# A decoder layer's mixer: heads spread by transfers, column groups filled across two chunks, squares added on GpSimd, the front a stage of its own

## The chip, the cores and the metric

The kernel runs on one core of a Trainium2 chip. The metric is the device time of one execution in microseconds (us). Three runs of the kernel before gave 1148.04, 1148.34 and 1158.81 us, with a median of 1148.34. One more execution was taken with the profiler.

## The reference

The input `x` has 16 batches of 256 positions and 256 channels, all float32. One layer applies three blocks, each followed by a layernorm of the sum with its input.

```python
# 1. mixer (32 heads k of 8 channels; 4 angles theta each)
z = causal_conv4(x @ in_proj_w)                  # x_val 256, gate 256, score 32
p_w = exp(clip(score_scale * z_score, -20, 20)) * time_weight
poly = w0 + w1 * x_val - w2 * x_val**2           # w = softmax(deriv_logits)
phi = x_val * theta
num_re, num_im, den = cumsum over t of p_w*poly*cos(phi), p_w*poly*sin(phi), p_w
re, im = num_re / max(den, 1e-4), num_im / max(den, 1e-4)
rs = rsqrt((sum(re**2) + sum(im**2)) / 64 + 1e-5)     # one per head and position
y = re*rs*norm[:32] @ W_re + im*rs*norm[32:] @ W_im
x = layernorm(x + (y * silu(z_gate)) @ out_proj_w)
# 2. attention by autocorrelation: 256-point spectra of q, k, v (16 heads), the
#    best delays of the mean correlation, softmax over them, v rolled and summed
x = layernorm(x + attn(x, ctx) @ Wo + bo)
# 3. feed-forward, a forward and an inverse branch of 8 experts of rank 64
h = gelu(q @ router_w1.T + b1); weights = softmax(h @ router_w2.T + ...)
out = sum_k weights_k * (xV_k * cumsum_t(yW_k)) @ U_k + weights @ b
x = layernorm(x + (fwd + alpha * inv) @ W_O.T)
```

## The kernel before

**Tiling.** Batches go in eight pairs. The mixer works with channels in the partitions and two batches of 256 positions in the free dimension. The feed-forward weights are multiplied together once at the start (`fold_weights`).

**The mixer.** `front` transposes `x`, forms the scores (line 208) and, from them, `pw`, the weight per head and position; heads lie in 16 rows of each 32-row group. It projects `x` in four blocks (line 225) and convolves them into `zcs` on VectorE (`convolve`, line 186). For the two value blocks `m` it builds `g`, the polynomial times `pw`. `pw` has a row for each head, and `g` one for each of 8 channels, so two products with a 0/1 matrix `sel_h` (line 231) copy each head's row to 8 rows of PSUM.

`body` takes each value block `m` in two chunks `h`. For a chunk it spreads channels to four angle rows by transfers (`spread`, line 247), forms sine and cosine in tiles `sn` and `cs`, multiplies by the spread `ge`, and sums over time with scans (`cumsums`, line 120). ScalarE squares both sums into `ge` and `sq` (279, 280). TensorE then forms `y` (line 284: weights of 32 columns, so a product fills one of four column groups of the array; a chunk `h` uses groups 2h and 2h+1) and adds the squares into `ss` (line 289: four groups; one set of products for `ge`, one for `sq`). The tiles `sn`, `cs` and `ge` have two buffers each. After both blocks, `sv`, the inverse of the norm, is copied from heads to channels by `sel_h` again (line 307), multiplied in (308), and projected out (316).

**Attention and feed-forward.** `attention` takes spectra (450), products (473, 484), picks delays in `choose`, rolls (`rolled`, 564, 574). `feed_forward` transposes, sums over time, forms router logits (611, 613, 614), softmax, then eight expert tiles `e` (two products at 661 and 665, a transfer `wb` of the weights, two VectorE multiplies 662 and 666), and at the end multiplies all eight with `u_o` (675) and the bias (676).

**What sets the order.** `run` interleaves generators: each stream has a start time, a length and a number of steps, and the one that is least advanced emits next. `mixer(p)`, body of pair p and then front of pair p+1, fills 70 steps from time p to p+1; attention of p starts at p+1.2, feed-forward at p+2.6. A planner then orders each engine's queue from this priority, its own estimates, and the free buffers; every queue runs in order. Eight pairs share nine `x` buffers. All transfers named here are issued by SyncE (SP).

Of the kernel before, what the change touches and what calls it, by code (L numbers as in the profile page):

```python
# [11 lines left out]
F32 = mybir.dt.float32  # L12
# [7 lines left out]
P = 128  # L20
B, L, D = 16, 256, 256
K, H, M, A = 32, 8, 4, 4
HM = H * M
# [11 lines left out]

A_AT, A_LEN = 0.2, 1.0
# [17 lines left out]
def decoder_kernel(ctx: ExitStack, tc: tile.TileContext, a: dict, out: bass.AP):  # L54
# [45 lines left out]
    sel_h = load("sel_h", [P, 2, D], eng=G)  # L100
# [89 lines left out]

    def front(p, made):
# [30 lines left out]
        for m in range(4):  # L222
            ps = m_bank()
            for c in range(2):
                T.matmul(ps, w_in[:, c, m * P : (m + 1) * P], xT[:, c, :, :], start=c == 0, stop=c == 1)  # L225
            zcs.append(convolve(mx, "zc", split(ps), m, 6))
            if m < 2:
                g = mx.tile([P, 2, L], F32, name="g", tag="g", bufs=3)
                ps = m_bank()
                for j in range(2):  # L230
                    T.matmul(
                        ps[:, j * L : (j + 1) * L], sel_h[:, j, m * P : (m + 1) * P], pw, start=True, stop=True
                    )
                S.activation(g, zcs[m], AF.Identity, bias=dw[:, 1:2], scale=dw[:, 3:4])
                G.tensor_tensor(g, g, zcs[m], ALU.mult)
                V.scalar_tensor_tensor(g, g, dw[:, 0:1], split(ps), ALU.add, ALU.mult)  # L236
                gs.append(g)
            if m < 3:
                yield 4
# [9 lines left out]
    def body(p, made):  # L249
        zcs, gs, den = made.pop(p)  # L250
        ss = y_ps.tile([P, L], F32, name="ss", tag="ss")
        for m in range(2):
            y = y_ps.tile([P, 512], F32, name="y", tag="y")
            for h in range(2):
# [22 lines left out]
                yield 5  # L277
                sq = mx.tile([P, 2, 512], F32, name="sq", tag="sq", bufs=1)
                S.activation(ge, sn, AF.Square)  # L279
                S.activation(sq, cs, AF.Square)  # L280
                for n, part in enumerate((cs, sn)):
                    for i in range(2):
                        q = 32 * (2 * h + i)
                        T.matmul(y[q : q + 32, :], w_ri[:, n, :], part[:, i, :], start=n == 0, stop=n == 1)  # L284
                for n, s in enumerate((ge, sq)):
                    for par in range(2):
                        for j in range(2):
                            q = 32 * (2 * par + j)
                            T.matmul(  # L289
                                ss[q : q + 32, :], ones_bd[:, 4 * m + 2 * h + par, :],  # L290
                                s[:, par, j * L : (j + 1) * L],
                                start=m == 0 and h == 0 and n == 0, stop=m == 1 and h == 1 and n == 1,
                            )
                yield 2
# [8 lines left out]
        for m in range(2):  # L303
            y = zcs[2 + m]
            ps = m_bank()
            for j in range(2):
                T.matmul(ps[:, j * L : (j + 1) * L], sel_h[:, j, m * P : (m + 1) * P], sv, start=True, stop=True)
            V.tensor_tensor(y, y, split(ps), ALU.mult)
# [110 lines left out]
    def mixer(p):  # L419
        if 2 * p + 2 < B:  # L420
            for b in (2 * p + 2, 2 * p + 3):
                if xs[b] is None:
                    load_x(b)
        yield from body(p, made)
        if p + 1 < NP:
            yield from front(p + 1, made)

    with tc.tile_pool(name="fold", bufs=1) as fold:
        for b in range(2, 4):
            load_x(b)  # L430
        run((0, 1, 70, mixer(0)))
# [160 lines left out]
    def feed_forward(p):  # L592
# [14 lines left out]
        for br in range(2):  # L607
            for rb in range(2):
# [3 lines left out]
                h = ff.tile([P, 512], F32, name="h", tag="h", bufs=2)  # L612
                S.activation(h, ps, AF.Gelu, bias=pv[:, C_RB1 + rb : C_RB1 + rb + 1])  # L613
                T.matmul(pl[32 * br : 32 * br + 32, :], w2t[:, rb, :], h, start=rb == 0, stop=rb == 1)  # L614
# [36 lines left out]
        es = []  # L651
        for br in range(2):
            for kb in range(4):
# [4 lines left out]
                e = ff.tile([P, 512], F32, name="e", tag="e", bufs=8)  # L658
# [10 lines left out]
        tiles = []  # L669
        for j in range(2):  # L670
            ps = f_bank()
            for c in range(2):
                o, cut = ps[:, c * D : (c + 1) * D], slice((2 * j + c) * P, (2 * j + c + 1) * P)
                for i in range(8):
                    T.matmul(o, es[i][:, cut], u_o[:, i, :], start=i == 0, stop=False)  # L675
                T.matmul(o, wT[:, cut], b_o, start=False, stop=True)  # L676
                yield 4
            V.tensor_tensor(pair[j], pair[j], split(ps), ALU.add)
            tiles += [pair[j][:, 0, :], pair[j][:, 1, :]]
# [6 lines left out]
    streams = [(p, 1.0, 70, mixer(p)) for p in range(1, NP)]  # L686
# [7 lines left out]
_HEADS = [[4 * cb + i for cb in range(par, 8, 2) for i in range(4)] for par in range(2)]  # L694
# [7 lines left out]
def _shape_constants():  # L702
# [27 lines left out]
    dist_p, sel_h = np.zeros((P, L)), np.zeros((P, 2, D))  # L730
    for q, rows in _score_rows():
        dist_p[rows] = dist[_HEADS[q // 2]]
        for r, k in zip(rows, _HEADS[q // 2]):
            sel_h[r, q % 2, k * H : (k + 1) * H] = 1.0
    c["dist"], c["sel_h"] = dist_p, sel_h
    ones_bd = np.zeros((P, 8, 32))
    for r in range(P):
        for cb in range(8):
            ones_bd[r, cb, 4 * (cb // 2) + r // HM] = 1.0
# [77 lines left out]
```

## Time and profile before

| What | us |
|---|---|
| median of three runs | 1148.34 |
| the profiled execution, its own time | 1144.82 |
| its span | 1143.0 |
| PE busy | 971.6 |
| DVE busy | 718.1 |
| ACT busy | 520.8 |
| POOL busy | 235.1 |

The span runs from the first to the last instruction; the rest of the profiled execution's time lies around it. PE is TensorE's matmuls, PEld its weight loads, DVE is VectorE, ACT is ScalarE, POOL is GpSimd, SP is SyncE. In a group, the line and engine come first, then output and inputs by name, the shape, the count, the busy time, the mean of one in nanoseconds, and the idle time of the engine before them with what ended it. A float32 product appears as two records. In a timeline the start comes first, then the length. Busy time says how long an engine worked and not who was late.

### The profile page before, as it was taken

The page shows a single profiled execution, that of the slowest core. Times are in us where ns is not written, and L with a number is a line of the kernel's source. Part 1 is how long each engine was busy: PE and PEld are TensorE (multiplying, and loading weights), DVE is VectorE, ACT ScalarE, POOL GpSimd, SP SyncE. Part 2 cuts the span into 40 slices and gives each one's busy share as a digit, 9 for nine tenths or more (in the row PEclk, how much of TensorE's full clock was granted, in tenths as well). Part 3 has the DMA queues.
Part 4 walks back from the last instruction along what each step waited for, and adds up shares of the span by engine and source line. Part 5 has one row for each costly group of instructions (what it writes and reads, how often), then busy time and mean ns, then how long its engine had stood idle before and what let it go on. Part 6 is the DMA issues. An engine that isn't in the chain of part 4 may idle for free.

```text
span 1143.0 us, 11089 instructions
## 1 busy us (share of the span) xinstructions
PE 971.6 (85%) x3820; PEld 543.0 (48%) x3820; DVE 718.1 (63%) x1197; ACT 520.8 (46%) x754; POOL 235.1 (21%) x499
## 2 busy tenths in 40 slices
PE   5868848767999788988999899988999799889695
PEld 2335315423547354553547454644456357356344
DVE  4866887865977578855886488855875443243231
ACT  2864774764654373633653474526463311310300
POOL 4102203212211320232112221122013211210100
PEclk9989968979999999998999899999999899989898
DMA  9612313310641143411550155203340050031050
GB/s 319 169 38 60 90 44 66 66 35 1 125 79 37 37 106 43 82 46 23 107 102 10 38 112 81 47 28 78 61 93 19 0 74 1 19 56 19 18 74 19
DMA packets 45512, 72.06 MB, mean 63 GB/s; under 512 B 4448, under 2 KB 18320, under 8 KB 45456
## 3 DMA queue, kind: packets, MB, share of 16 engines
q1 hardware_dynamic: 44240, 68.04, 29.1%
q0 software_dynamic: 1216, 3.31, 0.9%
q8 instruction: 30, 0.49, 0.2%
q14 instruction: 26, 0.21, 0.1%
HBM read 16.81 MB, written 4.19 MB: 18 GB/s over the span
## 4 chain that ended last, share of the span: by engine, by line
PE 49%; DVE 18%; POOL 7%; ACT 7%; issue 6%; DMA 1%; SPq 0%; POOLq 0%; ACTq 0%; DVEq 0%
PE fps L675 10%; PE fps L661 8%; PE fps L665 7%; PE y L284 3%; DVE zc L186 3%; ACT x L177 2%; PE mps L316 2%; DVE cs L120 2%; PE fps L473 2%; PE fps L450 2%; PE ss L289 2%; PE fps L614 2%; PE fps L574 2%; PE fps L611 1%; PE fps L676 1%
## 5 line engine op out<-in xcount | busy, mean ns | idle before, releaser
L661 PE MATMUL fps<-fcT,w_c 128*128 128x512 f32 x256 | 126.2, 617 | 0.0
L665 PE MATMUL fps<-fxT,w_v 128*128 128x512 f32 x256 | 120.4, 592 | 0.0
L675 PE MATMUL fps<-u_o,e 128*128 128x256 f32 x512 | 116.3, 380 | 0.0
L675 PEld LDWEIGHTS fps<-u_o,e 128*128 128x128 f32 x512 | 96.4, 190 | 18.1 <-issue 5.9
L170 POOL TENSOR_TENSOR ln_rs<-ln_rs 128x4 f32<-128x4 f32 x72 | 14.4, 199 | 440.9 <-DVE ln_rs L168 437.1
L177 ACT ACTIVATE x<-x,ln_rs 128x256 f32<-128x256 f32 x96 | 50.0, 592 | 113.6 <-POOL ln_rs L175 113.6
L611 PE MATMUL fps<-fxT,w_h 128*128 128x512 f32 x128 | 66.3, 643 | 18.8 <-ACT fxT L602 18.8
L665 PEld LDWEIGHTS fps<-fxT,w_v 128*128 128x128 f32 x256 | 49.2, 192 | 62.6 <-issue 58.8
L473 PE MATMUL fps<-Wkv,spec 128*128 128x512 f32 x128 | 64.4, 643 | 15.4 <-ACT spec L454 15.4
L186 DVE SCALAR_TENSOR_TENSOR zc<-mps,pv,zc 128x510 f32<-128x510 f32 (+2 forms) x96 | 70.4, 738 | 9.2 <-ACT zc L184 8.7
L120 DVE TENSOR_TENSOR_SCAN sn<-again,sn 128x1024 f32<-128x1024 bf16 x32 | 73.1, 2285 | 0.5
L120 DVE TENSOR_TENSOR_SCAN cs<-again,cs 128x1024 f32<-128x1024 bf16 x32 | 73.1, 2283 | 0.1
L661 PEld LDWEIGHTS fps<-fcT,w_c 128*128 128x128 f32 x256 | 48.4, 197 | 49.5 <-issue 48.6
L225 PE MATMUL mps<-xT,in_proj_w 128*128 128x512 f32 x128 | 68.3, 660 | 4.0 <-DVE g L236 4.0
L490 POOL TENSOR_TENSOR pp<-qf,kf 128x512 f32<-128x512 f32 x16 | 28.2, 1764 | 189.5 <-ACT qf L488 189.5
L279 ACT ACTIVATE ge<-sn 128x1024 f32<-128x1024 f32 x32 | 33.7, 1054 | 71.2 <-DVE sn L120 49.6
L662 DVE TENSOR_TENSOR e<-wb,fps 128x512 f32<-128x512 f32 x64 | 43.7, 682 | 34.3 <-PE fps L661 19.1
L289 PE MATMUL ss<-ge,ones_bd 128*32 128x256 f32 x256 | 47.4, 409 | 19.2 <-ACT ge L279 19.2
L265 ACT ACTIVATE sn<-sn,theta_col 128x512 f32<-128x512 f32 x64 | 45.9, 721 | 36.0 <-DMA sn<-zc 35.8
L666 DVE TENSOR_TENSOR e<-e,fps 128x512 f32<-128x512 f32 x64 | 43.7, 682 | 27.1 <-PE fps L665 25.9
L613 ACT ACTIVATE h<-fps,pv 128x512 f32<-128x512 f32 x32 | 21.2, 681 | 79.9 <-PE fps L611 79.9
L284 PE MATMUL y<-cs,w_ri 128*32 128x512 f32 x128 | 43.6, 660 | 12.8 <-DVE cs L120 11.5
(236 smaller groups left out, 1869.7 us busy)
## 6 DMA issues: line engine op xcount, KB each, us to landing
sn<-zc SPq DMA_DIRECT2D x64, 256.0 KB, 4.7
ge<-g SPq DMA_DIRECT2D x64, 256.0 KB, 4.9
wb<-fwT SPq DMA_DIRECT2D x64, 256.0 KB, 4.4
x<-in_x SPq DMA_DIRECT2D x16, 256.0 KB, 3.3
ct<-in_ctx SPq DMA_DIRECT2D x16, 256.0 KB, 2.7
out<-x SPq DMA_DIRECT2D x16, 256.0 KB, 2.1
in_proj_w<-in_in_proj_w SPq DMA_DIRECT2D x1, 512.0 KB, 6.2
V_fwd<-in_V_fwd SPq DMA_DIRECT2D x1, 512.0 KB, 11.2
```

What stands on the lines that cost most here:

```text
L120: V.tensor_tensor_scan(dst, again[:, : dst.shape[1]], src, 0.0, ALU.mult, ALU.add)
L177: S.activation(t, t, AF.Identity, scale=y[:, i : i + 1], bias=nb[:, i : i + 1])
L186: V.scalar_tensor_tensor(zc[..., s:], ps[..., : L - s], cw[:, 3 - s : 4 - s], zc[..., s:], ALU.mult, ALU.add)
L225: T.matmul(ps, w_in[:, c, m * P : (m + 1) * P], xT[:, c, :, :], start=c == 0, stop=c == 1)
L265: S.activation(sn[:, i, :], sn[:, i, :], AF.Identity, scale=tcol[:, cb : cb + 1])
L284: T.matmul(y[q : q + 32, :], w_ri[:, n, :], part[:, i, :], start=n == 0, stop=n == 1)
L289: T.matmul(ss[q : q + 32, :], ones_bd[:, 4 * m + 2 * h + par, :], s[:, par, j * L : (j + 1) * L], start=m == 0 and h == 0 and n == 0, stop ...
L473: T.matmul(ps, cf[:, c, f * P : (f + 1) * P], wkv[:, c, :], start=c == 0, stop=c == 1)
L611: T.matmul(ps, w_h[:, c, br, rb * P : (rb + 1) * P], xT[:, c, :, :], start=c == 0, stop=c == 1)
L661: T.matmul(pc, w_c[:, c, br, cut], cT[:, c, :, :], start=c == 0, stop=c == 1)
L665: T.matmul(pv_, w_v[:, c, br, cut], xT[:, c, :, :], start=c == 0, stop=c == 1)
L675: T.matmul(o, es[i][:, cut], u_o[:, i, :], start=i == 0, stop=False)
```

## The change

It has five parts.

1. `sel_h` and its four products per value block and pair are gone. `spread_heads` makes four transfers for each block, each taking 8 head rows and writing every row 8 times, into a tile `hs` with two buffers. It serves `pw` in the front and `sv` in the body. The order of heads in the groups (`_HEADS`, `ones_bd`) is changed to suit.
2. The body keeps `cs` and `sn` of both chunks and forms `y` after the second, over four column groups.
3. GpSimd adds the two squares of a chunk, and `ss` has half as many products.
4. Both branches' router projections are formed before their logits, so two logits products on different groups can follow each other; `h` has three buffers in place of two.
5. The front is a stream of its own, from p+0.3 to p+0.95, beside the body of the pair ahead. Besides these, the feed-forward multiplies by `u_o` after each branch of four experts, adding to `x` twice, and `e` has six buffers in place of eight.

```diff
+FRONT_AT, FRONT_LEN = 0.3, 0.65
-    sel_h = load("sel_h", [P, 2, D], eng=G)
+    def spread_heads(src, m):
+        t = mx.tile([P, 2, L], F32, name="hs", tag="hs", bufs=2)
+        for h in range(2):
+            for j in range(2):
+                q = 32 * (2 * (1 - h) + j) + 8 * m
+                nc.sync.dma_start(
+                    out=t[64 * h : 64 * h + 64, j, :], in_=src[q : q + 8].unsqueeze(1).to_broadcast([8, 8, L])
+                )
+        return t
...
-                ps = m_bank()
-                for j in range(2):
-                    T.matmul(
-                        ps[:, j * L : (j + 1) * L], sel_h[:, j, m * P : (m + 1) * P], pw, start=True, stop=True
-                    )
+                pe = spread_heads(pw, m)
...
-                V.scalar_tensor_tensor(g, g, dw[:, 0:1], split(ps), ALU.add, ALU.mult)
+                V.scalar_tensor_tensor(g, g, dw[:, 0:1], pe, ALU.add, ALU.mult)
...
+            parts, sqs = [], []
...
+                parts.append((cs, sn))
                 sq = mx.tile([P, 2, 512], F32, name="sq", tag="sq", bufs=1)
                 S.activation(ge, sn, AF.Square)
                 S.activation(sq, cs, AF.Square)
-                for n, part in enumerate((cs, sn)):
+                G.tensor_tensor(ge, ge, sq, ALU.add)
+                sqs.append(ge)
+                yield 1
+
+            for n in range(2):
+                for h in range(2):
                     for i in range(2):
                         q = 32 * (2 * h + i)
-                        T.matmul(y[q : q + 32, :], w_ri[:, n, :], part[:, i, :], start=n == 0, stop=n == 1)
-                for n, s in enumerate((ge, sq)):
-                    for par in range(2):
-                        for j in range(2):
-                            q = 32 * (2 * par + j)
-                            T.matmul(
-                                ss[q : q + 32, :], ones_bd[:, 4 * m + 2 * h + par, :],
-                                s[:, par, j * L : (j + 1) * L],
-                                start=m == 0 and h == 0 and n == 0, stop=m == 1 and h == 1 and n == 1,
-                            )
-                yield 2
+                        T.matmul(y[q : q + 32, :], w_ri[:, n, :], parts[h][n][:, i, :], start=n == 0, stop=n == 1)
+            for par in range(2):
+                for h in range(2):
+                    for j in range(2):
+                        q = 32 * (2 * (1 - h) + j)
+                        T.matmul(
+                            ss[q : q + 32, :], ones_bd[:, 4 * m + 2 * h + par, :],
+                            sqs[h][:, par, j * L : (j + 1) * L],
+                            start=m == 0 and par == 0, stop=m == 1 and par == 1,
+                        )
+            yield 2
...
-            ps = m_bank()
-            for j in range(2):
-                T.matmul(ps[:, j * L : (j + 1) * L], sel_h[:, j, m * P : (m + 1) * P], sv, start=True, stop=True)
-            V.tensor_tensor(y, y, split(ps), ALU.mult)
+            V.tensor_tensor(y, y, spread_heads(sv, m), ALU.mult)
...
-        run((0, 1, 70, mixer(0)))
+        run((0, 1, 48, body(0, made)), (FRONT_AT, FRONT_LEN, 22, early_front(1)))
...
-        for br in range(2):
-            for rb in range(2):
+        for rb in range(2):
+            hs = []
+            for br in range(2):
...
-                h = ff.tile([P, 512], F32, name="h", tag="h", bufs=2)
+                h = ff.tile([P, 512], F32, name="h", tag="h", bufs=3)
                 S.activation(h, ps, AF.Gelu, bias=pv[:, C_RB1 + rb : C_RB1 + rb + 1])
-                T.matmul(pl[32 * br : 32 * br + 32, :], w2t[:, rb, :], h, start=rb == 0, stop=rb == 1)
+                hs.append(h)
+            for br in range(2):
+                T.matmul(pl[32 * br : 32 * br + 32, :], w2t[:, rb, :], hs[br], start=rb == 0, stop=rb == 1)
...
+            for j in range(2):
+                ps = f_bank()
+                for c in range(2):
+                    o, at_ = ps[:, c * D : (c + 1) * D], slice((2 * j + c) * P, (2 * j + c + 1) * P)
+                    for i in range(4):
+                        T.matmul(o, es[i][:, at_], u_o[:, br * 4 + i, :], start=i == 0, stop=i == 3 and br == 1)
+                    if br == 0:
+                        T.matmul(o, wT[:, at_], b_o, start=False, stop=True)
+                    yield 2
+                V.tensor_tensor(pair[j], pair[j], split(ps), ALU.add)
...
-    streams = [(p, 1.0, 70, mixer(p)) for p in range(1, NP)]
+    streams = [(p, 1.0, 48, body(p, made)) for p in range(1, NP)]
+    streams += [(p - 1 + FRONT_AT, FRONT_LEN, 22, early_front(p)) for p in range(2, NP)]
```

`early_front(p)` loads the two batches of pair p if they are not loaded yet and runs `front(p)`.

More of the change, by code (lines that the diff above doesn't have):

```diff
@@ L417, in fold_weights, with early_front @@
         V.tensor_copy(b_o, ps[:, :D])
[L419 to L426, printed above, removed]
+    def early_front(p):
+        for b in (2 * p, 2 * p + 1):
+            if xs[b] is None:
+                load_x(b)
+        yield from front(p, made)
     with tc.tile_pool(name="fold", bufs=1) as fold:
@@ L649, in feed_forward @@
         yield 2
-        es = []
         for br in range(2):
+            es = []
             for kb in range(4):
@@ L657, in feed_forward @@
                 nc.sync.dma_start(out=wb, in_=wT[lo : lo + 16].unsqueeze(1).to_broadcast([16, 8, 512]))
-                e = ff.tile([P, 512], F32, name="e", tag="e", bufs=8)
+                e = ff.tile([P, 512], F32, name="e", tag="e", bufs=6)
                 pc = f_bank()
@@ L668, in feed_forward @@
                 yield 5
[L669 to L679, printed above, removed]
+            for j in range(2):
[8 more added lines that the diff above has]
+                V.tensor_tensor(pair[j], pair[j], split(ps), ALU.add)
+        tiles = [t[:, c, :] for t in pair for c in range(2)]
         layernorm(ff, "fl", tiles)
@@ L689, in decoder_kernel @@
     run(*streams)
-_HEADS = [[4 * cb + i for cb in range(par, 8, 2) for i in range(4)] for par in range(2)]
+_HEADS = [[4 * cb + i for cb in range(8) if cb % 4 // 2 == h for i in range(4)] for h in (1, 0)]
 def _score_rows():
@@ L729, in _shape_constants @@
     dist = np.where(np.arange(K)[:, None] < K - A, (L - 1) - t[None, :], t[None, :])
-    dist_p, sel_h = np.zeros((P, L)), np.zeros((P, 2, D))
+    c["dist"] = np.zeros((P, L))
     for q, rows in _score_rows():
[L732 to L735, printed above, removed]
+        c["dist"][rows] = dist[_HEADS[q // 2]]
     ones_bd = np.zeros((P, 8, 32))
@@ L738, in _shape_constants @@
         for cb in range(8):
-            ones_bd[r, cb, 4 * (cb // 2) + r // HM] = 1.0
+            ones_bd[r, cb, 4 * (2 * (cb // 4) + cb % 2) + r // HM] = 1.0
     c["ones_bd"] = ones_bd
```

## The prediction

> **What bounds the kernel now.** I read the busy times of the page first, then the windows of one pair, then the groups of the instructions concerned, then timelines where two engines meet. The page, and the windows between two equal points of successive pairs (columns: length, then busy time of PE, PEld, DVE, ACT, POOL, then the granted clock, DMA share, GB/s):
>
> ```profile
> PE 971.6 (85%) x3820; PEld 543.0 (48%) x3820; DVE 718.1 (63%) x1197; ACT 520.8 (46%) x754; POOL 235.1 (21%) x499
> ```
>
> ```profile
> 376.00:502.00 126.00, 112.46 (x466) 63.35 (x465) 88.56 (x146) 63.14 (x90) 28.43 (x60) 0.99 0.32 63
> 502.00:546.00 44.00, 34.58 (x136) 18.87 (x135) 24.17 (x57) 20.34 (x37) 10.31 (x22) 0.92 0.22 52
> 546.00:627.20 81.20, 78.71 (x329) 44.79 (x328) 64.03 (x89) 42.75 (x53) 17.59 (x38) 1.00 0.37 70
> ```
>
> A pair of batches costs 125.5 us (normalised rows of line 177 start at 376.46, 502.44, 627.97, 752.39 and 877.93 in the chain). In 81 us of it PE is full; in the other 44 us the chains of front, logits and choice meet, and PE has 9 us idle. PE has some 114 us of work per pair, DVE 88.5. Five such pairs lie between 254 us, where the first feed-forward begins, and 878; the start (0 to 254: PE 182, DVE 184 busy) and the tail (878 to the end) are bound otherwise.
>
> The matmuls that the change touches, from the groups:
>
> ```profile
> L284 PE MATMUL y<-cs,w_ri 128*32 128x512 f32 x128 | 43.6, 660 | 12.8 <-DVE cs L120 11.5 <-DVE ln_rs L168 0.9 <-DVE m L512 0.4
> L231 PE MATMUL mps<-sc,sel_h 128*128 128x256 f32 x64 | 22.0, 475 | 20.1 <-DVE top L520 13.4 <-DVE sc L215 4.2 <-DVE g L236 2.5
> L307 PE MATMUL mps<-sv,sel_h 128*128 128x256 f32 x64 | 20.1, 471 | 4.2 <-DVE sv L302 4.1
> L614 PE MATMUL fps<-h,w2t 128*32 128x512 f32 x64 | 34.1, 618 | 15.3 <-ACT h L613 15.3
> ```
>
> Each product is two records. Products on the full array start 0.86 us apart at 512 columns, 0.43 at 256. The timeline of one chunk's y and ss shows what a column group is worth:
>
> ```profile
> 604.71 1.05 PE L284 MATMUL y<-cs,w_ri 128*32 128x512 f32 x4
> 605.59 0.60 PE L284 MATMUL y<-sn,w_ri 128*32 128x512 f32 x2
> 606.70 0.78 PE L289 MATMUL ss<-sq,ones_bd 128*32 128x256 f32 x6
> 607.41 3.72 PE L675 MATMUL fps<-u_o,e 128*128 128x256 f32 x16
> ```
>
> Two y products on two groups take 0.88 us (604.71 to 605.59), as one alone would, and six ss records on four groups share 0.78; y and ss of a chunk together take 2.70 (604.71 to 607.41).
>
> **What the Trainium skill says.** "TensorEngine Tiling (Array Packing)", Key Properties: tiles work independently. Agrees: the two y above. "GPSIMD Engine Reference", Specifications: GpSimd shares its SBUF interfaces with DVE instructions that have two SBUF inputs. Agrees, from the POOL and DVE timelines:
>
> ```profile
> 609.99 2.17 POOL L490 TENSOR_TENSOR pp<-qf,kf 128x512 f32<-128x512 f32 x1 [21.00 <-ACT qf L488]
> ```
>
> ```profile
> 608.81 2.28 DVE L120 TENSOR_TENSOR_SCAN cs<-again,cs 128x1024 f32<-128x1024 bf16 x1
> 611.01 1.44 DVE L492 SCALAR_TENSOR_TENSOR pp<-qf,kf 128x256 f32<-128x256 f32 x1
> ```
>
> The POOL product (1.26 us when alone, at 507.57) lasts 2.17 and ends 1.1 us after the scan; the DVE product (0.42 alone, at 505.11) lasts 1.44, past POOL's end. They take turns. "TensorE: Matmul & The Clock Gate", What's actually happening: after an idle window PE runs at half clock. Agrees: after 6.50 us idle, eight c_corr records take 3.62 us (149.80) where they otherwise take about 2. "DMA: Bandwidth & Descriptors", Anatomy of one DMA: about 2.0 us fixed; the 256 KB spreads here land in 4.7, no 64 KB one is shown.
>
> **Part by part, per steady pair.**
>
> *Removed from PE.* sel_h: 8 products of 256 columns, 8 x 0.43 = 3.4. y: per m, four rounds of 0.86 on two groups become two on four. The planned order issues m=0 whole, but puts one product of m=1 ahead on its own: 1.72 + 0.86 = 2.6. ss: half the products, 2 x 0.86 = 1.7. Logits: four rounds become two, 1.7 (in the tail the order puts projections between them and little is left). Sum 9.4: PE's floor is 114 - 9.4 = 104.5.
>
> *Added.* u_o in two halves: the same products, two more adds on DVE, 2 x 0.68 = 1.4. Four POOL adds of 128x1024: 512 elements take 1284 ns at line 465, so 2.57 each, 10.3; POOL goes from 28 to 38, and its Newton steps queue behind an add. Turns with DVE: no row shows such an add; between 0 (in a DVE gap) and 2.5 us each, I take 1.0, 4 in all. DVE: 88.5 + 1.4 + 4 = 94. Sixteen hs transfers on SP: issues of 0.6 us, 10 per pair, ahead of ge and wb; landing between 2.0 (the page) and 4.7 (the 256 KB row), I take 3.5. The front's four hide behind convolutions; the body's need sv's reciprocal, then hs buffers that the front's g must free, and DVE waits about 2 us for them, with the next e products queued behind.
>
> *Buffers.* cs, sn and ge (two each) are now held by both h until y and ss of the m. So at each m the next spread starts only after that: two issues of 0.65, landing 4.7, ACT 0.72 + 1.15 = 7.9 us, against some 6 us of DVE work that the order puts between (qf, pp, prod, e). 2 us of DVE idle, twice; behind it wait e products, and PE's u_o behind those.
>
> *The front as its own stage, and the sum of a pair.* In the steady order the front hardly moves: its second x still waits for an output tile to leave (9 x buffers for four pairs in flight). What moves is the body's end: out-projection and layernorm, today ahead of the e products, stand among them. I split a pair at the last u_o product and at the first e product. Before: 495.4 to 545.8 = 50.4, and 545.8 to 621.0 = 75.2.
>
> First stretch after: PE has 23 us of rounds in it and is not the bound. The path: from the last u_o product to its add on DVE 5 (DVE has more ahead of it than before), the statistics with the fcT scan and two body products between them 8.5, Newton on POOL behind half a pp product 5, four normalised tiles on ACT 2.4, the output's issue and transfer 1.4 + 2.1, the new x 0.6 + 3.3, then transpose, score, projection and choice up to the first e 7. Sum 35.
>
> Second stretch after, PE's rounds counted off the order: e 8 x 3.44 = 27.5, u_o and b_o 36 x 0.43 = 15.5, attention's two outputs 6.9, projections 5.2, out-projection 3.4, transforms with kv and q 12.2, y and ss 2.6, an x transpose 0.9: 74. Stalls, read off the rows by adding the durations of what each engine has ahead: 4 where a half's last u_o round waits for its e (DVE has 36 us of rows up to it, PE 30), 2 at out-projection for hs, 3 where the fourth projection waits for a PSUM bank that the convolutions free late, 4 at the second transform behind the scans, 2 where u_o waits behind the buffers: 15. From the 89 I take 4, since DVE instructions start 0.08 closer than they last (0.60 apart at 0.68) and some fifty of them are on the path: 85.
>
> Pair: 35 + 85 = 120 against 125.5, **5.5 saved**, of the 9.4 that PE loses. Ends: 112 (33, and 5 us of stalls in the second) and 130 (38, and 92 with POOL's turns at 2.5).
>
> *Start, tail.* Front 1 and 2 no longer stand whole between bodies (94.75 to about 128 before), but DVE, 62 busy of 80 there, keeps its work: 10 saved, from -10 to 20. Tail: three logits at 0.86, 3.
>
> Sum: 5 x 5.5 + 10 + 3 = 40. Span 1143.0 to 1103; own time 1144.8 to 1104.8. The median of the runs is 3.5 above the profiled one: **1108**.
>
> **Rivals.** (1) *PE's saving arrives whole.* For: PE full in 81 of 125 us; gaps of front and body fill each other. Against: DVE at 94 of 112. Pair 112: 5 x 13.5 + 13 = 80, 1068. (2) *Slower, by the shared buffers.* Each of 16 ends of an m costs DVE the whole refill because prod and e, which I let cover it, come late themselves (prod waits for POOL, which now takes turns). Price 4 us more at each, 64 in all: 1172. It decides from 40 / 16 = 2.5 us on. For: the refill of 7.9 is hidden today by free buffers (line 265 waits for DMA only 1.2 us a time); PE idling would add half clock. Against: the other streams' work in the order. (3) *DVE takes PE's place*: the pair stays at 125, only start and tail gain, 1138.
>
> **Numbers.** Forecast 0.45, (1) 0.20, (2) 0.22, (3) 0.13. One per cent is 11.5 us, about what a measurement of this kernel tells from none. Faster: forecast and (1), 0.65; slower: (2), 0.22; the rest same. The range goes from 1064, just under case (1), to 1172, the middle of case (2), leaving a tenth on each side.
>
> **What would show it.** The sel_h rows gone; y records down from four rounds to two in a run of eight; distance of line 178's normalised rows about 120; DVE idle before the cs product after each m near 2 us, (2) if above 4; POOL's adds near 2.6 alone and longer beside scans; hs landing under 4 us. Wrong if the wait of the front's second x, or PE clock under 0.9 in the pairs, eats the 9.4.

## The result and the profile after

The changed kernel takes **1215.07 us** in the median (1212.03 to 1216.13) against 1148.45 for the kernel before, run beside it: a ratio of 1.0553, 95% interval 1.0491 to 1.0615. The forecast was 1108, and faster. The profiled execution has a span of 1213.4 us against 1143.0.

First the busy times of the page, for the changed kernel:

```profile
PE 948.1 (78%) x3436; PEld 527.9 (44%) x3436; DVE 738.1 (61%) x1213; ACT 527.9 (44%) x762; POOL 351.5 (29%) x530
```

PE lost 24 us of busy time (971.6 before) and 384 records; only POOL gained much (235.1 before). No engine is fuller than PE was, so the 70 us are not the work of a fuller engine: engines wait for each other more. The chain that ended last says where. Its shares by engine, for the kernel before and then for the changed one:

```profile
PE 49%; DVE 18%; POOL 7%; ACT 7%; issue 6%; DMA 1%; SPq 0%; POOLq 0%; ACTq 0%; DVEq 0%
```

```profile
PE 32%; DVE 23%; POOL 13%; DMA 10%; ACT 8%; issue 7%; SPq 6%; POOLq 0%; DVEq 0%; ACTq 0%
```

PE's own work was half of the chain and is a third now; DVE, GpSimd, transfers and SP's issues stand in its place. The first transposes of the feed-forward (line 610) start at 258.07, 389.45, 525.18, 662.57, 799.85 and 939.57, those of the kernel before (line 601) at 254.03, 375.66, 501.65, 627.19, 751.61 and 877.14: the start is 4 us longer, five pairs take 681.5 us where they took 623.1, and the rest 8 more. The window of a pair before, then of a pair of the changed kernel and of the next pair's two stretches as the prediction cuts them (length, busy PE, PEld, DVE, ACT, POOL, granted clock, DMA share, GB/s):

```profile
502.00:627.50 125.50, 113.59 (x466) 63.97 (x465) 88.39 (x146) 63.09 (x90) 28.12 (x60) 0.97 0.32 63
389.45:525.18 135.73, 111.26 (x417) 62.51 (x416) 88.52 (x148) 62.68 (x91) 44.86 (x63) 0.91 0.33 66
525.18:563.20 38.02, 27.90 (x130) 12.96 (x129) 24.66 (x47) 20.96 (x36) 13.60 (x20) 0.91 0.09 28
563.20:662.57 99.37, 82.72 (x288) 48.83 (x287) 64.85 (x102) 41.88 (x56) 31.25 (x44) 0.93 0.42 80
```

The first stretch is 38.0 (forecast 35), the second **99.4 (forecast 85)**; it was 75.2 before. A pair has 48 PE records less (466 to 418), which is the sel_h and ss products that were removed, and DVE has about what it had (88.5 and 89.5 for 88.4). PE idles 24 to 27 us of a pair instead of 12.

Who waits for what, from the list of waits (us in all, times, longest), the changed kernel first and then the kernel before:

```profile
ACT x L178 <- POOL ln_rs L176: 200.7, 24, 50.8
ACT sn L274 <- DMA sn<-zc: 93.5, 38, 8.5
PE fps L626 <- ACT h L623: 36.0, 14, 3.9
DVE zc L320 <- DMA hs<-sv: 32.1, 14, 5.5
PE mps L328 <- DVE zc L320: 27.9, 9, 5.9
DVE g L244 <- DMA hs<-sc: 25.8, 11, 4.0
DVE cs L277 <- ACT cs L276: 8.0, 3, 4.1
```

```profile
ACT x L177 <- POOL ln_rs L175: 113.6, 24, 50.6
ACT sn L265 <- DMA sn<-zc: 35.8, 30, 2.8
DVE cs L268 <- ACT cs L267: 16.0, 8, 2.9
PE fps L614 <- ACT h L613: 15.3, 10, 2.9
PE mps L316 <- DVE zc L308: 9.5, 5, 2.4
```

The waits for hs are new. `DVE cs` is the wait that the forecast named for the shared buffers, 2 us at each of 16 ends of an m: it is 8.0 us in all. A wait that grew is not yet a loss: ACT's wait for GpSimd's ln_rs, the largest here, is 171.4 us in `k_core` below, which is faster than the kernel before. The groups concerned (busy, mean ns of one, idle time before and its cause):

```profile
L291 POOL TENSOR_TENSOR ge<-ge,sq 128x1024 f32<-128x1024 f32 x32 | 84.4, 2639 | 199.9 <-ACT sq L290 199.9
L171 POOL TENSOR_TENSOR ln_rs<-ln_rs 128x4 f32<-128x4 f32 x72 | 37.7, 524 | 251.8 <-DVE ln_rs L169 248.0
L299 PE MATMUL y<-cs,w_ri 128*32 128x512 f32 x128 | 34.6, 689 | 23.2 <-DVE cs L121 19.5 <-DVE ln_rs L167 2.9 <-DVE ln_rs L169 0.6
L626 PE MATMUL fps<-h,w2t 128*32 128x512 f32 x64 | 36.2, 769 | 36.0 <-ACT h L623 36.0
```

The add lasts about what the forecast said (a mean of 2.64 us for 2.57). The first instruction of a Newton round on GpSimd (each layernorm refines its inverse root in three such rounds of four small instructions) has a mean of 524 ns. Before, it was:

```profile
L170 POOL TENSOR_TENSOR ln_rs<-ln_rs 128x4 f32<-128x4 f32 x72 | 14.4, 199 | 440.9 <-DVE ln_rs L168 437.1
```

The timelines of GpSimd and DVE in the second stretch show what became of it:

```profile
615.99 2.36 POOL L291 TENSOR_TENSOR ge<-ge,sq 128x1024 f32<-128x1024 f32 x1 [3.14 <-ACT sq L290]
618.32 2.26 POOL L474 TENSOR_TENSOR x<-x,bo 128x512 f32<-128x512 f32 x1
620.53 2.18 POOL L171 TENSOR_TENSOR ln_rs<-ln_rs 128x4 f32<-128x4 f32 x1
622.79 1.10 POOL L172 TENSOR_TENSOR ln_rs<-ln_rs 128x4 f32<-128x4 f32 x1
623.98 2.17 POOL L173 TENSOR_SCALAR ln_rs<-ln_rs 128x4 f32<-128x4 f32 x1
626.23 0.20 POOL L174 TENSOR_TENSOR ln_rs<-ln_rs 128x4 f32<-128x4 f32 x1
```

```profile
616.89 2.55 DVE L282 TENSOR_TENSOR sn<-sn,ge 128x1024 f32<-128x1024 f32 x1 [1.56 <-ACT sn L278]
619.96 2.76 DVE L121 TENSOR_TENSOR_SCAN sn<-again,sn 128x1024 f32<-128x1024 bf16 x1
622.64 1.19 DVE L283 TENSOR_TENSOR cs<-cs,ge 128x1024 f32<-128x1024 f32 x1
623.87 2.29 DVE L121 TENSOR_TENSOR_SCAN cs<-again,cs 128x1024 f32<-128x1024 bf16 x1
```

A GpSimd step on 4 columns that starts beside a scan ends with the scan (620.53 + 2.18 and 619.96 + 2.76; 623.98 + 2.17 and 623.87 + 2.29). ACT, which waits for the last step, has the squares and the next chunk's sine and cosine behind it. SP's timeline shows the issues of the transfers:

```profile
572.94 8.09 SPq L198 DMA_DIRECT2D hs<-sc  x8
581.07 0.57 SPq L255 DMA_DIRECT2D sn<-zc  x1
581.81 4.30 SPq L198 DMA_DIRECT2D hs<-sv  x4
586.22 0.65 SPq L255 DMA_DIRECT2D ge<-g  x1
586.98 4.05 SPq L198 DMA_DIRECT2D hs<-sv  x4
```

Sixteen issues take 16.4 us, 1.0 each where the forecast has 0.6; a ge issue stands between them.

### The profile page after: what moved, and what is told of

It is laid out like the page before. It is cut to its first block, busy times and chain, and to the rows that moved or that the text cites. A ratio compares the mean times of both kernels' runs of the same rounds, so it can differ in the third digit from the quotient of the medians.

```text
span 1213.4 us, 10541 instructions
## 1 busy us (share of the span) xinstructions
PE 948.1 (78%) x3436; PEld 527.9 (44%) x3436; DVE 738.1 (61%) x1213; ACT 527.9 (44%) x762; POOL 351.5 (29%) x530
## 4 chain that ended last, share of the span: by engine, by line
PE 32%; DVE 23%; POOL 13%; DMA 10%; ACT 8%; issue 7%; SPq 6%; POOLq 0%; DVEq 0%; ACTq 0%
PE fps L673 5%; SPq L198 5%; PE fps L677 5%; DVE sn L121 4%; PE fps L686 4%; DMA sn<-zc 3%; POOL ln_rs L171 3%; PE y L299 2%; DVE sn L282 2%; POOL ge L291 2%; PE fps L482 2%; ACT x L178 2%; DVE cs L121 2%; DVE cs L283 2%; POOL ln_rs L173 2%
## 5 line engine op out<-in xcount | busy, mean ns | idle before, releaser
L673 PE MATMUL fps<-fcT,w_c 128*128 128x512 f32 x256 | 142.5, 686 | 0.0
L291 POOL TENSOR_TENSOR ge<-ge,sq 128x1024 f32<-128x1024 f32 x32 | 84.4, 2639 | 199.9 <-ACT sq L290 199.9
L686 PE MATMUL fps<-u_o,e 128*128 128x256 f32 x512 | 123.4, 387 | 15.7 <-DVE e L678 12.0
L171 POOL TENSOR_TENSOR ln_rs<-ln_rs 128x4 f32<-128x4 f32 x72 | 37.7, 524 | 251.8 <-DVE ln_rs L169 248.0
L673 PEld LDWEIGHTS fps<-fcT,w_c 128*128 128x128 f32 x256 | 55.6, 223 | 49.2 <-issue 46.8
L187 DVE SCALAR_TENSOR_TENSOR zc<-mps,pv,zc 128x506 f32<-128x506 f32 (+2 forms) x96 | 69.6, 736 | 10.3 <-ACT zc L185 10.0
L328 PE MATMUL mps<-out_proj_w,zc 128*128 128x256 f32 x128 | 38.9, 456 | 33.4 <-DVE zc L320 27.9
L626 PE MATMUL fps<-h,w2t 128*32 128x512 f32 x64 | 36.2, 769 | 36.0 <-ACT h L623 36.0
L282 DVE TENSOR_TENSOR sn<-sn,ge 128x1024 f32<-128x1024 f32 x32 | 51.6, 1612 | 18.6 <-ACT sn L278 18.5
L482 PE MATMUL fps<-Wkv,spec 128*128 128x512 f32 x128 | 60.1, 611 | 2.7 <-ACT spec L463 2.7
```

The costliest lines, as they stand in the source:

```text
L171: G.tensor_tensor(t, y, y, ALU.mult)
L187: V.scalar_tensor_tensor(zc[..., s:], ps[..., : L - s], cw[:, 3 - s : 4 - s], zc[..., s:], ALU.mult, ALU.add)
L282: V.tensor_tensor(sn, sn, ge, ALU.mult)
L291: G.tensor_tensor(ge, ge, sq, ALU.add)
L482: T.matmul(ps, cf[:, c, f * P : (f + 1) * P], wkv[:, c, :], start=c == 0, stop=c == 1)
L673: T.matmul(pc, w_c[:, c, br, cut], cT[:, c, :, :], start=c == 0, stop=c == 1)
```

## The experiments

Theories: **T1**, the transfers (issue and landing) are the loss; **T2**, cs, sn and ge are held until both chunks' products are done, and the next spread comes late; **T3**, the GpSimd add, its turns with DVE and what queues behind; **T4**, the front as its own stage, which moves layernorm and out-projection among the scans. Later a fifth: the order, that is, which instructions meet in the queues. Each ratio below is to the kernel before, run beside it.

### One part undone in the changed kernel

```diff
# u_sel: heads by products again (front shown; the same with sv in body)
-                pe = spread_heads(pw, m)
+                ps = m_bank()
+                for j in range(2):
+                    T.matmul(ps[:, j * L : (j + 1) * L], sel_h[:, j, m * P : (m + 1) * P], pw, start=True, stop=True)
# u_chunk: y at each chunk, inside the loop over h; ss of the chunk in the same way, on two groups
-                        T.matmul(y[q : q + 32, :], w_ri[:, n, :], parts[h][n][:, i, :], start=n == 0, stop=n == 1)
+                        T.matmul(y[q : q + 32, :], w_ri[:, n, :], part[:, i, :], start=n == 0, stop=n == 1)
# x_noadd
-                G.tensor_tensor(ge, ge, sq, ALU.add)
# u_front (the first streams shown; the later ones in the same way)
-        run((0, 1, 48, body(0, made)), (FRONT_AT, FRONT_LEN, 22, early_front(1)))
+        run((0, 1, 70, mixer(0)))
```

> The changed kernel, with the heads spread by sel_h products on PE again instead of 16 transfers per pair. T1 (the hs transfers are the main cause: in the profile of the changed kernel SP spends 8.1 us on eight hs issues and 8.4 us on the next eight, each lands 4.2 to 4.4 us later, and DVE and the out-projection wait 5.5 to 5.9 us for them): two such waits with their issues, some 8 us per pair, come back, 8 pairs: about 1150 to 1165. T2 (buffers held by both chunks), T3 (the GpSimd add and what queues behind it) and T4 (front as its own stage): 3.4 us of PE come back per pair and little else changes: 1200 to 1230.

> The changed kernel, with the products y and ss formed at the end of each chunk again (y on two column groups at a time, ss on the two groups of its chunk), so that cs, sn and ge come free per chunk; the GpSimd add stays. T2 (the refill after each m, 10.9 us from the last y product to the next scan against 7.9 in the forecast, sets the time): the refill is hidden again, about 5 us at each of 16 ends of an m, 80 at most: 1140 to 1180. T1, T3, T4: PE pays 2.6 us more per pair and the y products still wait for the add: 1205 to 1230.

> The changed kernel without the 32 GpSimd adds of squares: the squares of cs are left out of the sum, all else stays. T3 (the add takes turns with the scans, delays the Newton steps on GpSimd, and with them the ACT queue, where squares and the next spread stand): the squares reach PE 4 us earlier at each chunk and the scans shorten from 2.3 to 2.2 us; some 6 us per pair and the start's share: 1150 to 1175. T1, T2, T4: only the add's own 2.6 us leave a path where they are partly hidden: 1200 to 1215.

> The changed kernel, with the front back inside the mixer's stream (one stream of 70 steps, body of a pair and then front of the next). T4 (the separate stage moves the body's layernorm and out-projection among the scans, so that GpSimd's Newton steps of 0.2 us take 2.1 beside a scan and ACT stands behind them): the Newton steps go back to 0.2 us, 6 to 8 us per pair: 1155 to 1170. T1, T2, T3: transfers, buffers and adds stay: 1200 to 1225.

Measured: u_sel 1175.14 (1.0209, 1.0174 to 1.0244), u_chunk 1203.88 (1.0449, 1.0418 to 1.0479), x_noadd 1178.75 (1.0234, 1.0203 to 1.0264), u_front 1238.38 (1.0751, 1.0721 to 1.0781). Undoing T1 brings 40 us, leaving out the add 36, undoing T2 11. T4 falls: without the stage the kernel is 23 us slower, although the first Newton instruction is back at a mean of 211 ns, which the expectation had priced at 6 to 8 us per pair. (Its steady pairs are 133.2 us instead of 137.5, so the stage does cost there; but the start, where the first two marks are 176 us apart instead of 131, loses far more.) u_sel, which lies between its two expected ranges, keeps the changed order of heads; only the transfers are undone in it.

### The rest alone, and parts added to it

k_core is the kernel before with the stage, the logits and u_o in halves. If the parts add up, it takes 1215 - 40 - 36 - 11 = 1128.

```diff
# k_core, a_front: to the kernel before (k_core with the diff's logits and u_o lines too)
-    streams = [(p, 1.0, 70, mixer(p)) for p in range(1, NP)]
+    streams = [(p, 1.0, 48, body(p, made)) for p in range(1, NP)]
+    streams += [(p - 1 + FRONT_AT, FRONT_LEN, 22, early_front(p)) for p in range(2, NP)]
# k_core_y: to k_core, after the loop over h
+            for n in range(2):
+                for h in range(2):
+                    for i in range(2):
+                        q = 32 * (2 * h + i)
+                        T.matmul(y[q : q + 32, :], w_ri[:, n, :], parts[h][n][:, i, :], start=n == 0, stop=n == 1)
# a_add: to the kernel before
+                G.tensor_tensor(ge, ge, sq, ALU.add)
-                for n, s in enumerate((ge, sq)):
```

> The kernel before with three parts of the change alone: front as its own stage, logits side by side, u_o in two halves; sel_h products, y and all squares at each chunk as before, no GpSimd add. T1 with T3 (hs transfers and the GpSimd add, worth 40 and 36 us when each alone was undone, are the loss, and the rest of the change gains): the undone parts add up, 1215 - 40 - 36 - 11 = 1128, within 10. T4' (these three parts cost too, since the body's layernorm and out-projection now stand among the scans): 1150 to 1170. If the two undone parts hid behind each other (each takes away the same wait), then more remains: 1165 to 1180.

> As the kernel with front, logits and u_o halves alone, and y of both chunks formed together on four column groups, so that cs and sn are held until the end of an m; ge and the squares come free per chunk, no add. T2 (held buffers cost more than four groups give): slower than the kernel without it by 10 us or more, since the next sn spread waits for y. If the loss in y's grouping lay in the wait for the add: PE's 2.6 us per pair come through, 5 to 15 us faster than without it.

> The kernel before with front as its own stage and nothing else of the change. The forecast's step: 10 us gained in the start, pairs as before: about 1138 (1128 to 1168). T4' (in the steady pair the layernorm among the scans costs some 4.7 us, as the pairs of 137.9 against 133.2 us of the changed kernel with and without it suggest, while the start gains up to 50): 1148 - 40 + 5 x 4.7 = about 1132. If the stage only pays because the transfers need cover: 1145 to 1165.

> The kernel before with GpSimd's add of squares alone (ss from the sum, half as many ss products, still at each chunk; y as before). T3 (the add's 2.6 us before the products, its turns with DVE's two-input products): 1170 to 1185, as much as leaving it out gained in the changed kernel. T1 or T2 (the add hurts only where buffers are held until the end of an m): 1140 to 1160.

Measured: k_core **1129.32 (0.9824, 0.9773 to 0.9874)**, a_front **1130.72 (0.9826, 0.9776 to 0.9877)**, k_core_y 1166.04 (1.0139, 1.0085 to 1.0192), a_add 1171.93 (1.0182, 1.0140 to 1.0224). The stage alone gains 1.7%; logits and halves add nothing that can be told from it. Both kernels beat the kernel before and the changed one. The add alone, on the kernel before, costs 1.8%, within what was expected of it, though a steady pair there stays at 126.4 us. The window of a pair of k_core shows that the stage gains nothing there:

```profile
620.40:746.80 126.40, 113.27 (x466) 64.08 (x464) 87.54 (x147) 66.23 (x93) 28.66 (x60) 0.97 0.32 63
```

The pair is what it was (125.5). The first feed-forward begins at 231.8 instead of 254.0, but that lead of 22 us does not last: at the second mark (368.5 for 375.7) it is 7, and 4 at the sixth (873.2 for 877.1). The other 17 us of k_core's profiled execution are gained after that, in the tail. In a_front the lead is 22 at the first mark, 12 at the second (363.5), 8 at the sixth (869.0) and 11 at the end. That 1128 was met looked like a sum that adds up, but y's grouping costs 37 us here where undoing it brought 11. So the other two were added in the same way, and T2's refill and T3's place were tried by themselves.

```diff
# k_hs: to k_core, with the changed layout of heads (ss of a chunk on the two groups of h)
+            V.tensor_tensor(y, y, spread_heads(sv, m), ALU.mult)
-                            q = 32 * (2 * par + j)
+                            q = 32 * (2 * (1 - h) + j)
# k_add: to k_core
+                G.tensor_tensor(ge, ge, sq, ALU.add)
# t_sn3: to k_core_y (and logits in the old order, h bufs=2)
-                sn = mx.tile([P, 2, 512], F32, name="sn", tag="sn", bufs=2)
+                sn = mx.tile([P, 2, 512], F32, name="sn", tag="sn", bufs=3)
# u_dve: to the changed kernel
-                G.tensor_tensor(ge, ge, sq, ALU.add)
+                V.tensor_tensor(ge, ge, sq, ALU.add)
```

> The three parts front, logits and u_o halves (1129 us) with the heads spread by transfers in place of sel_h products; y and all squares at each chunk, no add (a chunk's squares on the two groups of its heads, which adds four rounds of 0.43 us per pair to PE). T1 (the transfers cost by themselves: SP's issues of 0.8 to 1.0 us and DVE's wait of 4 to 6 us for a landing): 1129 + 40 = 1165 to 1175, as much as undoing them gained in the changed kernel. If they cost only where another wait meets them (next to held buffers, y's grouping on top of them adds but 11 us with the add present, 37 without both): 1135 to 1150.

> The three parts front, logits and u_o halves (1129 us) with GpSimd's add of squares and half the ss products, still at each chunk. T3 (add alone, place by place): as on the kernel before, about 19 us: 1145 to 1155. If the separate stage makes it worse (layernorm's steps on GpSimd now stand behind the add): 1160 to 1170, the 36 us that leaving it out gained in the changed kernel.

> As the kernel with front, u_o halves and y of both chunks together (1166 us with side-by-side logits), but with three sn buffers instead of two, so that the next sn transfer need not wait for the y products of the m; room for it is made by the old logits order with two h buffers. T2 (the refill after each m is what y's grouping costs: two issues and a landing of 4.7 us, 16 times): most of the 37 us return, 1130 to 1145. If y's grouping costs by where its products stand in PE's order, or by cs alone: 1155 to 1170.

> The changed kernel with the 32 adds of squares on VectorE instead of GpSimd. T3 (turns between GpSimd and VectorE, and ss behind a 2.6 us add): VectorE's add lasts about 1.2 us and takes no turns; the queue of VectorE grows by 32 x 1.21 = 39 us, some of it idle time today: 1185 to 1205. If VectorE's order is what sets the pair: 1215 to 1245.

Measured: k_hs 1221.92 (1.0570, 1.0519 to 1.0621), k_add 1179.11 (1.0215, 1.0183 to 1.0247), t_sn3 1174.35 (1.0185, 1.0154 to 1.0216), u_dve 1203.86 (1.0431, 1.0398 to 1.0465). k_hs, k_add and, by 4 us, t_sn3 are slower than either of their expected ranges.

Three things follow. First, **the three parts do not add up**. With k_core and the changed kernel as the two ends, all eight combinations are there (medians). They are not quite clean: x_noadd leaves half of the squares out; every kernel with transfers also has the changed order of heads, and of those without only u_sel has it; with that order, squares added at each chunk use two groups and take more rounds (k_hs, u_chunk).

| y grouped | add | transfers | us | kernel |
|---|---|---|---|---|
| no | no | no | 1129 | k_core |
| yes | no | no | 1166 | k_core_y |
| no | yes | no | 1179 | k_add |
| no | no | yes | 1222 | k_hs |
| yes | yes | no | 1175 | u_sel |
| yes | no | yes | 1179 | x_noadd |
| no | yes | yes | 1204 | u_chunk |
| yes | yes | yes | 1215 | changed kernel |

The transfers cost 93, 25, 13 or 40 us, the add 50, 9, -18 or 36, the grouping 37, -4, -43 or 11, by what else is there (9 and -4 cannot be told from nothing: the intervals overlap). Each alone more than undoes the 20 us that the stage gains; together they cost 86.

Second, the refill of sn is not what the grouping costs. With a third sn buffer the next sn spread need not wait for y, and t_sn3 is no faster. In its list of waits ACT now stands at cs, of which there are two:

```profile
ACT cs L269 <- PE y L298: 23.1, 5, 4.6
ACT sn L267 <- DMA sn<-zc: 17.0, 19, 3.3
```

The wait for the sn transfer was no longer in k_core_y either (17.2 us in all). What cs and sn both wait for is the y product, and that stands in PE's queue behind whatever the order has put ahead of it: in the chain of k_core_y PE runs without a gap from 718 to 747 us, the y products last, and the issue, the landing of 5.1 us and ACT follow. A third cs buffer was not tried, so what holding cs costs stays open.

Third, moving the add to DVE brings only 11 us (u_dve), of the 36 that leaving it out brings. Whether the rest is the hand-over between squares and ss, on either engine, or the work that DVE takes on in u_dve, these runs do not separate.

### The transfers taken apart

```diff
# k_hs0: to k_hs, logits in the old order, both spreads by products (as in u_sel)
-            V.tensor_tensor(y, y, spread_heads(sv, m), ALU.mult)
+            V.tensor_tensor(y, y, split(ps), ALU.mult)
# k_hsF: to k_hs0, front only
+                pe = spread_heads(pw, m)
# k_hsB: to k_hs0, body only
+            V.tensor_tensor(y, y, spread_heads(sv, m), ALU.mult)
# u_hsact: to the changed kernel, in spread_heads
-                nc.sync.dma_start(
+                (nc.sync, nc.scalar)[j].dma_start(
```

> Front as its own stage and u_o in two halves, old logits order, the changed kernel's layout of the heads and a chunk's squares on the two groups of its heads, but heads spread by sel_h products: the kernel with transfers (1222 us) less its transfers. T1 (the transfers are the cost): four more rounds of 0.43 us per pair and nothing else against 1130: 1130 to 1155. Rival (the two-group squares are the cost, not the transfers): 1180 to 1215.

> As k_hs0, with the front's heads spread by transfers, the body's by sel_h products. In the chain of the kernel with both, a pair holds 11.9 us of SP's hs issues, 4.1 us of landing for the front's and 4.9 for the body's. T1 by issues (each of 16 costs the same): half of the difference between k_hs0 and 1222. T1 by the forecast's reading (the front's hide behind the convolutions, the body's do not): 5 to 10 us above k_hs0.

> As k_hs0, with the body's heads spread by transfers, the front's by sel_h products. T1 by issues: half of the difference between k_hs0 and 1222, as for the front's. T1 by the forecast's reading (only the body's wait on the path): nearly the whole difference.

> The changed kernel, with two of the four transfers of each hs tile issued from ScalarE's queue instead of SP's. If SP's issue time is what costs (11.2 us per pair in the chain that ended last, eight issues in a row): half of it leaves the chain, 4 us per pair or more: 1170 to 1190. If the landing of 4.3 us and the waits for it cost: 1200 to 1220. If ScalarE's queue, which then stands behind the wait for the scores and for sv's reciprocal, pays instead: 1220 to 1245.

Measured: k_hs0 1175.46 (1.0210, 1.0158 to 1.0262), k_hsF 1197.59 (1.0391, 1.0350 to 1.0431), k_hsB 1159.11 (1.0068, 1.0049 to 1.0088), u_hsact 1215.70 (1.0543, 1.0496 to 1.0589).

Half of the 93 us is not the transfers: k_hs0 has the changed order of heads but no transfer, and is 45 us slower than k_core or a_front. A chunk's eight products of squares take four rounds on two groups instead of two on four, so eight more rounds of 0.43 us per pair, 3.4, and by estimate 28 in eight pairs (the expectations' four rounds are miscounted; PE busy of a pair rose by 3.6). What makes up the rest of the 45 is not shown. The front's transfers cost 22, the body's **gain** 16, and both together cost 46 (k_hs, which also has the new order of logits). The forecast said that the front's hide and the body's do not; here it is the other way round. k_hsF fits the expectation by issues (half of the difference), which k_hsB then refutes.

In the changed kernel's chain SP's hs issues make up 11.2 us of the pair that begins at 662.5 (the pieces of the chain in that window summed). With half of them on ACT's queue they make up 2.6, and the pair stays at 137.4 us. The chain's shares by engine for u_hsact:

```profile
PE 33%; DVE 25%; DMA 13%; POOL 10%; ACT 9%; issue 5%; SPq 2%; ACTq 1%; POOLq 0%; DVEq 0%
```

SP went from 6% to 2%, and DMA, DVE and ACT took its place: ACT, which now issues half of the transfers, is idle 22.5 us in all before the cs of line 276 and 17.4 before the zc of line 185 until an hs transfer, which it was not before. So a share of the chain was not a price that could be had back. Whether the issue time would be worth something on a queue with nothing behind it stays open.

### The same operations at another place

If a part's price changes its sign with its neighbours, the order may set it. One number each moves attention and feed-forward by a twentieth of a pair against the body:

```diff
-A_AT, A_LEN = 0.2, 1.0
-F_AT, F_LEN = 1.6, 1.0
+A_AT, A_LEN = 0.25, 1.0
+F_AT, F_LEN = 1.65, 1.0
```

> The changed kernel with attention and feed-forward 0.05 of a pair later against the body (starts of 0.25 and 1.65 in place of 0.2 and 1.6); every operation is the same. If the size of the loss belongs to the parts (transfers, add, held buffers): 1205 to 1225, only the start moves by some 6 us. If it belongs to the meeting of queues in the written order: over 15 us to either side, below 1200 or above 1230.

> Front, logits and u_o halves alone (1129 us) with the same shift of 0.05 of a pair. If the parts set the time: 1125 to 1140. If the meeting of queues does: over 15 us slower, since its pair of 126.3 us holds PE's 113 us of work with 13 us of stalls that the old order happens to keep short.

Measured: ph_after 1249.22 (1.0855, 1.0792 to 1.0919), ph_core 1167.72 (1.0142, 1.0089 to 1.0196). No operation was added, and both lose: 34 and 38 us, as much as y's grouping alone. The pair of ph_core:

```profile
640.57:773.64 133.07, 115.41 (x465) 65.80 (x464) 86.41 (x147) 62.67 (x90) 30.24 (x59) 0.95 0.31 60
```

Against k_core's 126.4 it has the same records, 4.5 us more PE idle and 2.1 more PE busy at a lower clock. The sum of the three parts, however, is hardly touched: 86 us at the old place, 82 at the new. Only this one shift, to one side, was tried; whether some other order would let the three parts gain stays open.

The windows of one steady pair, side by side (us; idle is length less PE busy):

| kernel | pair | PE busy | PE idle | clock |
|---|---|---|---|---|
| before | 125.5 | 113.6 | 11.9 | 0.97 |
| k_core | 126.4 | 113.3 | 13.1 | 0.97 |
| k_hsB | 129.8 | 112.7 | 17.1 | 0.95 |
| u_sel | 131.5 | 111.4 | 20.1 | 0.95 |
| ph_core | 133.1 | 115.4 | 17.7 | 0.95 |
| k_core_y | 133.6 | 114.2 | 19.4 | 0.94 |
| k_add | 133.7 | 112.9 | 20.8 | 0.94 |
| k_hs0 | 134.8 | 116.9 | 17.9 | 0.94 |
| changed | 137.3 | 110.0 | 27.3 | 0.93 |
| k_hsF | 140.2 | 117.8 | 22.4 | 0.89 |
| k_hs | 141.1 | 115.6 | 25.5 | 0.89 |
| ph_after | 146.2 | 112.4 | 33.8 | 0.88 |

Down the table the pair lengthens mostly by PE's idle time, and the granted clock falls roughly with it, so PE's busy time does not fall as its products do. (k_hsF stands out: 0.89 with less idle time than the changed kernel.)

## Why the prediction was wrong

**Where it failed.** The second stretch of the pair, "85", made of 74 us of rounds and 15 of stalls less 4. It measured 99.4: PE is busy in 82.7 of it and idle in 16.7. So 8.7 us are the rounds, and 5.7 are stalls (16.7 for 11). The rounds were counted at their full-clock distance: 82.7 at the granted 0.93 are an estimated 76.9 at full clock, so some 6 of the 8.7 are the clock, for which the sum had no term. With the first stretch (38.0 for 35) five pairs take 681.5 for 5 x 120, 81.5 of the 110 us between the forecast span and the measured one; the start (258 for 244) and the tail (274 for 263) have most of the rest.

**The stalls, term by term.** hs transfers: issue 1.0 in the row above for 0.6 (median of all 0.78, longest 1.98), landing 3.4 to 4.4 in the chain of two pairs for 3.5. (The 2.0 us that the prediction took as the lower end is stated in the Trainium skill, "DMA: Bandwidth & Descriptors", Anatomy of one DMA — SWDGE (gpsimd) path, for transfers that GpSimd issues; these are issued by SP.) In the pair that begins at 525.2, DVE waits 5.4 us for the body's hs for 2, and 4.7 for the front's for none (means over eight pairs: 4.0 and 3.2), and PE 6.0 for the out-projection's operand for 2. Logits: of their two pairs of products one was planned apart, so that 0.86 was saved for 1.7. PE waits 5.6 us in that pair for gelu (ACT h; 1.5 in a pair before), and 36.0 in all. The new order of logits is not enough to cause that: k_core has it too, with 7.5 in all, and k_hsB, with the old order, has 36.4 (k_core's line first):

```profile
PE fps L615 <- ACT h L612: 7.5, 5, 3.5
PE fps L621 <- ACT h L620: 36.4, 12, 4.8
```

DVE's total of 94 was wrong the other way, 87 to 91: the turns with the add cost DVE 0.38 us at the sn product (1.61 for 1.23), not 1.0.

**What the working left out.** Where the Newton steps stand. Lines 171 to 173 lasted 199, 200 and 194 ns and last 524, 349 and 375: 0.66 us more for each of 72 rounds, 47 us in all and 5.9 in a pair with three layernorms, in front of ACT. The prediction cited the shared interfaces (the Trainium skill, "GPSIMD Engine Reference", Specifications) and applied them to the new add and to the products; the 128x4 steps fall under the same rule beside a scan, which has two inputs (again and sn); the timelines above show it. x_noadd still has 453 ns at line 171 and a_add only 203, so it is not the add alone that delays them. But the 47 us are time on GpSimd and no price: u_front, with 211, 254 and 205 ns, is 23 us slower than the changed kernel, and ph_after, with 314, 241 and 198, is 34 us slower.

**What was right.** The add's 2.57 (mean 2.64, median 2.35, longest 4.37); the products that PE loses (48 records per pair; two rounds for y, 641.02 to 642.76 with all 16 records); the first stretch to 3 us, though in part by luck: after the normalised tiles its chain runs over gelu and the logits products (547.4 to 550.4), not over the output and the new x that the forecast had on the path; the refill after an m (y ends at 643.0, ACT has written cs at 651.4: 8.4 for 7.9; the 10.9 in an expectation above runs on to the sn product at 653.9 and was no fair comparison); and the start's gain by the stage alone (10 forecast; 7 in k_core and 12 in a_front by the second mark), which the other parts then took back. The clock in the pairs stayed above the 0.9 that the prediction had given as a warning.

The rival "slower by the shared buffers" had the right sign. Its mechanism is not borne out. DVE's idle time filed before the cs product, by which it was to be told, fell. Added up in DVE's timeline from the end of `zc<-zc,y` to the next cs product, in front of whatever instruction, it is 5.1 us at the first of the two ends of an m in a steady pair (0 before), which is above the rival's mark of 4; but it is 4.9 in k_core too, which frees its buffers at each chunk and is one of the two fastest kernels here. And a third sn buffer brought nothing back. What y's grouping costs (37 us alone) is not the refill's length; that it is when y's turn comes on PE, and what ACT and DVE have behind that, was read from one place of the chain and not tested. Two slips beside this: in the third rival start and tail gain 10 + 3, which gives 1135 and not 1138; and the GpSimd product at 507.57 was not alone, since a scan that started during it (507.96) lasted 3.02 us for 2.28, so there the one that started first kept its length.

**The deeper error.** The forecast priced each part by itself and added, with 9.4 us of PE to set against them. PE's 9.4 us are worth little here: of 7.9 us of full-clock work that left the pair (113.6 x 0.97 less 110.0 x 0.93, an estimate, since busy times are modelled) the lower clock took 4.3 back. And the prices are not the parts' own: the same transfers, with the order of heads that goes with them, cost 93 or 13 us, those of the body alone bring 16, and no operation at all, only a shift by a twentieth, 34 to 38. What is shown: the three parts together cost 82 to 86 us in two orders, four times what the stage gains. What stays open is a price for each: in these runs none could be given apart from what stood beside it. That the clock falls because PE stalls, and not the other way round, was only read from the table.

## What to carry to other kernels

When PE is nine tenths busy in a pair and the order is written out by hand, work taken off PE can cost more than its rounds if what replaces it adds a hand-over between engines: here products that fed the next step directly became transfers, an add on another engine and buffers released later, and PE idled twice as long. Try such parts one at a time, and try each at a second place in the order before believing its price. A longer wait or a larger share of the chain is not a price either: take it away and measure. Of the parts, the one that moved nothing to another engine and only gave a chain of its own to the front gained 1.7% alone.

## What the runs showed of the hardware that was not expected

A GpSimd instruction on 128x4 elements (0.20 us alone) that came up beside a DVE scan of 128x1024 ended with the scan in the rows above, after 2.18 us at line 171 and after 2.17 at line 173, which is a TENSOR_SCALAR with one tensor input; the longest of them in this run took 3.33 (line 172). Issues on SP did not go by size: the 64 KB hs issues have a median of 0.78 us, those of the 256 KB spreads 0.92 (sn) and 1.05 (ge), and single ones run from 0.54 to 1.98. And the granted clock of a steady pair ran from 0.97 to 0.88 over kernels whose PE busy time differs by 7%, lowest where PE idles most.
